# The stores of the results, issued from ScalarE's queue instead of SyncE's: a two-layer graph kernel on one Trainium2 core

## The chip, the cores and the metric

The kernel runs on one core of a Trainium2 chip. A core has five engines, each with an instruction queue of its own that is worked off in order: PE (TensorE, matrix products), DVE (VectorE), ACT (ScalarE), POOL (GpSimd) and SP (SyncE, which issues transfers and computes nothing). SP and ACT can both issue DMAs, and POOL issues the indirect ones. The metric is the device time of one execution in microseconds (us), lower is better.

## The reference

The input `x` has 32 batches of 512 channels by 1024 nodes, `adj` is 512 x 512, and everything is float32. Two graph layers follow each other, each with a residual and a normalisation over the nodes:

```python
q = einsum('c,bcn->bn', wq, x); k = einsum('c,bcn->bn', wk, x)
scores = leaky_relu(q[:, None, :] + k[:, :, None], 0.01)
att = softmax(scores, axis=-1)
agg = einsum('bcn,bmn->bcm', x, att)
x = layernorm(x + relu(einsum('oc,bcm->bom', adj, agg) + bm[None, :, None]))

W = support * adj            # as called here: adj * adj
x = layernorm(x + einsum('bnf,nm->bmf', x, W) + bias)
```

## The kernel before

The batches go through a software pipeline: in one pass of the list, `ld` works for the batch three ahead, `p`, `r`, `sd` and `fe` for the one two ahead, `t`, `e` and `pi` for the next, `u` and `m` for the current one, `st`, `av` and `so` for the one before. For one batch the steps are these; the short names are those of the kernel's own list.

- `ld0` to `ld3` (`load`, L131) bring the four channel tiles of x, 512 KB each, into one of three x buffers.
- `p0` to `p27` (`project`, L338) multiply x with the weights on PE; `k...` (`keep`) bring the products to `zrow`, on ACT or on DVE.
- The attention is not formed as a matrix. The scores depend on a sum of two numbers, so nodes are sorted by q: `r0` to `r7` (`place`, L403) count ranks on DVE, `sd` (`send`, L415) scatters the rows to their rank in a DRAM table `td` by indirect DMA on POOL, `fe` (`fetch`, L461 and L466) reads the sorted rows back into `zs`.
- `t0` to `t8` (`table`, L510) form running sums on PE, block by block. `e0` to `e8` (`table_out`, L522) copy each result out of PSUM on ACT. `ca` (on ACT) and `cp` (on POOL), both `carry` at L528, put the last row of a block into the next block, so that t(k+1) waits for e(k), ca(k) and cp(k). `ts` (`table_store`, L536) writes the sums back to the DRAM table from SP, two DMAs for each block.
- `pi` (`pick`, L543) gathers for each node its rows of the table, on POOL. `sc` (`scale`, L582) on ACT and `ga`, `gb` (`gain`, L587) on DVE mix them.
- `u`, `ad` (`add`, L603), `sq` (`square`, L611 and L612, on ACT), `rt` (POOL) and `y` (`finish`, L627 and L628, on ACT) turn the rows, add the residual and normalise.
- `m0` to `m13` (`multiply`, L676) are the second layer's products on PE, seven instead of eight by Strassen's scheme in Winograd's form, into the banks oA, oB and oC. `rd` (`read`, L697 and L699) brings them to `vall`, the one buffer for results in most rounds.
- `st`, `ro`, `sf` and `av` (`stats`, `root`, `shift`, `apply`, L705 to L729) normalise; `av0` to `av3` run on ACT, one for each of the four tiles of 128 x 1024. `so0` to `so3` (`store`, L734) write the four tiles to the output, 512 KB each. In the last batch, tiles 2 and 3 are normalised and stored in halves: `fa` (`apply_half`, half 0 on ACT, half 1 on DVE) and `fo` (`store_half`, L758).

The order of all this is written out by hand, as three lists of step names: BEGIN, SLOT and END. SLOT is run 28 times, each time with the roles moved on by one batch, and is called a round below. `with tc.manual_schedule()` keeps each engine's instructions in the order of the list; semaphores for data are added by the framework. In SLOT the stores stand here:

```python
k021 ga7 sc4 p19 sf1 gb1 e0 p17 ca0 ts0 sf2 cp0 sc6 x12 t1 av1 ga6 p16 gb6 e1 p18 wx1 cp1 ts1
ca1 wb1 p13 so1 k1p1 sc5 t2 ga4 gb7 p22 e2 x14 p23 ca2 k111 cp2 ga5 t3 k1u2 k1p5 gb5 p24 gb4 e3
ca3 u0 ts3 cp3 av2 so3 t4 ad0 so2 p21 so0 e4 ts2 ca4 u1 cp4 sq0 t5 ad1 p20 ld0 e5 ca5 u2 cp5 ts5
```

So in ACT's order the neighbours of so1 are ca1 and k1p1, and so3, so2 and so0 come one after the other between av2 and e4. In SP's order so1 stands between ts1 and ts3, and the other three between ts3 and ts2.

In the kernel before, all plain transfers are issued from SP, but for three small loads of vectors at the start (L76), which ACT issues.

Of the kernel before, what the change touches and what calls it, by code (L numbers as in the profile page):

```python
# [23 lines left out]
def gat_gcn_resnorm_kernel(  # L24
# [11 lines left out]
    nc = tc.nc  # L36
    P = 128
# [37 lines left out]
    for i, a in enumerate((wq, wk, bm)):  # L75
        nc.scalar.dma_start(  # L76
            out=vec[i * CT : (i + 1) * CT, :], in_=a.rearrange("(t p) -> t p", p=P)
# [9 lines left out]
    for half in range(2):  # L87
        p0 = half * G
        nc.gpsimd.affine_select(
            out=tri[p0 : p0 + G, 0, :], in_=tri[p0 : p0 + G, 0, :], pattern=[[-2, G]],  # L90
# [3 lines left out]
            out=tri[p0 : p0 + G, 1, :], in_=tri[p0 : p0 + G, 1, :], pattern=[[2, G]],  # L94
# [3 lines left out]
    for row, i in ((0, 0), (G, 1)):  # L98
# [14 lines left out]
        out=first, in_=first, pattern=[[-1, 2 * N - P]], compare_op=ALU.is_ge,  # L113
# [11 lines left out]
    xs, vs = {}, {}  # L125
# [16 lines left out]
    for td in tdb:  # L142
        nc.sync.dma_start(
            out=td.rearrange("(s u) c -> s u c", u=3)[N:NS, 0, :], in_=zs[P + N - NS : P, 0, 0:ZW]
        )
        odd = td.rearrange("(s w u) c -> s w (u c)", w=2, u=3)
        for r in range(0, NS // 2, P):
            n = min(P, NS // 2 - r)
            nc.sync.dma_start(
                out=odd[r : r + n, 0, ZW : 3 * ZW].rearrange("p (j c) -> p j c", j=2)[:, :, 0:1],  # L150
                in_=zs[0:n, 0:2, 1:2],
            )
            nc.sync.dma_start(
                out=odd[r : r + n, 1, ZW : 3 * ZW].rearrange("p (j c) -> p j c", j=2),
                in_=zs[0:n, 0:2, 0:ZW],
# [575 lines left out]
            by.tensor_scalar(t, t, rs, nb, ALU.mult, ALU.add)  # L731

    def store(b, mt):
        nc.sync.dma_start(out=out[b, mt * P : (mt + 1) * P, :], in_=vs[b][:, mt])  # L734

    parted = {}

# [17 lines left out]

    def store_half(b, mt, h):
        f = slice(h * H, (h + 1) * H)
        nc.sync.dma_start(out=out[b, mt * P : (mt + 1) * P, f], in_=vs[b][:, mt, f])  # L758

    steps = {}  # L760

# [38 lines left out]
    for ot in range(CT):  # L800
        also(0, f"u{ot}", turn, ot)
        also(0, f"ad{ot}", add, ot)
        also(0, f"sq{ot}", square, ot)
        also(0, f"rt{ot}", root0, ot)
        also(0, f"y{ot}", finish, ot)
        also(3, f"ld{ot}", load, ot)
        also(0, f"T{ot + 1}", less, ot + 1)
        also(-1, f"st{ot}", stats, ot)
        also(-1, f"ro{ot}", root, ot)
        also(-1, f"sf{ot}", shift, ot)  # L810
        also(-1, f"av{ot}", apply, ot)
        also(-1, f"so{ot}", store, ot)
# [8 lines left out]
    for mt in range(CT):  # L821
        also(0, f"ag{mt}", both, mt)
        for h in range(2):
            also(0, f"hb{mt}{h}", half, mt, h)
            also(0, f"fa{mt}{h}", apply_half, mt, h)
            also(0, f"fo{mt}{h}", store_half, mt, h)
# [150 lines left out]
```

## Time and profile before

| | |
|---|---|
| time, median of 3 runs | 2201.99 us (2200.96 to 2205.12) |
| the profiled execution | 2198.41 us |
| its span, first to last instruction | 2196.7 us |
| mean granted TensorE clock | 0.990 |
| HBM read, written | 338.17 MB, 208.30 MB |
| DMA queue q1 (SP) | 277.06 MB, 43.7% of 16 engines' span |
| DMA queue q0 (POOL) | 269.52 MB, 34.3% |
| DMA queue q10 (ACT) | 0.01 MB, 0.0% |

Times in the profile's lines are in us unless they are marked ns. In a timeline, a line has the start, the duration, the engine with the line of the kernel, the operation, what is written and read, how many instructions are merged, and in brackets the engine's idle time before it and who ended it. SPq and ACTq are the queues of these engines: issuing a DMA counts as no busy time of the engine. A DMA's duration there is that of the issue, not that of the transfer. L12 is line 12 of the kernel.

### The profile page before, as it was taken

What the parts mean: (1) busy time and instruction counts of PE and PEld (TensorE: products, weight loads), DVE (VectorE), ACT (ScalarE), POOL (GpSimd) and SP (SyncE); (2) the same over time, 40 slices, a digit from 0 to 9 for tenths busy, and PEclk for the clock granted to TensorE, in tenths of its full rate; (3) what the DMA queues carried; (4) which work ended last, traced back from release to release, by engine and by line L of the source; (5) the groups of instructions that cost most, each with busy time, mean ns of one, the idle gap of its engine ahead of it and who ended that gap; (6) DMA issues with size and microseconds to landing.
All of it is one profiled execution on the core that took longest, in us unless ns stands there. A gap on an engine that the chain in (4) does not pass through costs nothing.

```text
span 2196.7 us, 35479 instructions
## 1 busy us (share of the span) xinstructions
PE 2102.5 (96%) x11697; PEld 1222.4 (56%) x11697; DVE 1775.9 (81%) x3576; ACT 1652.8 (75%) x2758; POOL 987.6 (45%) x1291
## 2 busy tenths in 40 slices
PE   7879999999999999999999999999999999999877
PEld 5446555556555556555656555556655556655433
DVE  7567888888888888888888898888888888888666
ACT  1577777887777887777888777878777788777765
POOL 1344455444445444445443445544445544445442
PEclk9999999999999999999999999999999999999998
DMA  7567888878888777888777889887888887888752
GB/s 250 166 229 252 264 266 281 257 239 254 268 260 277 262 247 244 268 246 286 266 250 234 265 253 282 273 249 233 262 265 267 282 252 236 258 265 264 221 205 96
DMA packets 179152, 548.86 MB, mean 250 GB/s; under 512 B 27404, under 2 KB 27416, under 8 KB 178968
## 3 DMA queue, kind: packets, MB, share of 16 engines
q1 hardware_dynamic: 121600, 277.06, 43.7%
q0 software_dynamic: 57344, 269.52, 34.3%
q8 instruction: 93, 1.52, 0.3%
q14 instruction: 91, 0.75, 0.1%
q10 hardware_dynamic: 24, 0.01, 0.0%
HBM read 338.17 MB, written 208.30 MB: 249 GB/s over the span
## 4 chain that ended last, share of the span: by engine, by line
PE 62%; ACT 12%; DVE 10%; issue 6%; DMA 6%; POOL 3%; SPq 1%; DVEq 0%; POOLq 0%; ACTq 0%
PE zp_A L338 18%; PE tp L510 10%; PE oA L676 9%; PE zp_B L338 8%; PE op L596 5%; PE zp_C L338 4%; DVE junk L403 4%; ACT y L628 4%; PE oB L676 3%; PE oC L676 3%; DMA zs<-td 2%; ACT rows L582 2%; ACT v L699 1%; POOL zs L528 1%; DMA td<-zs 1%
## 5 line engine op out<-in xcount | busy, mean ns | idle before, releaser
L587 DVE SCALAR_TENSOR_TENSOR rows<-rows,ra 128x512 f32<-128x512 f32 x512 | 366.2, 739 | 20.9 <-ACT rows L582 17.6
L676 PE MATMUL oA<-y,adj_sb 128*128 128x512 f32 x768 | 356.6, 607 | 9.8 <-ACT y L628 6.3
L415 POOL DMA_INDIRECT td<-zrow,ranki x256 | 269.3, 1052 | 213.7 <-DVE idx L439 80.0
L510 PE MATMUL tp<-zs,lq 128*64 128x257 f32 x2304 | 335.1, 392 | 27.2 <-POOL zs L528 16.3
L543 POOL DMA_INDIRECT rows<-td,idx x256 | 297.1, 1160 | 88.1 <-issue 68.0
L403 DVE SCALAR_TENSOR_TENSOR junk<-qb,zrow,first 128x1024 int8<-128x1024 f32 x240 | 307.1, 1279 | 10.9 <-PE qb L376 4.2
L528 POOL COPY zs<-ts 1x513 f32<-1x513 f32 x128 | 93.2, 728 | 474.4 <-ACT ts L522 474.3
L338 PE MATMUL zp_A<-wb,x 128*64 128x257 f32 (+1 forms) x1536 | 278.9, 388 | 12.6 <-issue 3.5
L428 ACT ACTIVATE junk<-lq,kc 128x1024 int8<-128x1024 f32 x240 | 274.4, 1143 | 2.0
L603 DVE SCALAR_TENSOR_TENSOR y<-op,nbm,x 128x1024 f32<-128x1024 f32 x128 | 163.8, 1282 | 127.4 <-PE op L596 127.2
L676 PEld LDWEIGHTS oA<-y,adj_sb 128*128 128x128 f32 x768 | 144.7, 193 | 191.7 <-issue 153.8
L510 PEld LDWEIGHTS tp<-zs,lq 128*64 128x64 f32 x2304 | 168.7, 136 | 135.6 <-POOL zs L528 37.8
L582 ACT ACTIVATE rows<-rows,ra 128x512 f32<-128x512 f32 x256 | 180.1, 718 | 77.5 <-DVE den L574 39.5
L359 ACT COPY zrow<-zp_A 128x514 f32<-128x514 f32 x192 | 112.8, 588 | 147.4 <-PE zp_A L338 130.1
L338 PEld LDWEIGHTS zp_A<-wb,x 128*64 128x64 f32 (+1 forms) x1536 | 177.0, 155 | 77.3 <-issue 25.1
L528 POOL COPY zs<-zs 1x513 f32<-1x513 f32 x128 | 78.3, 611 | 253.0 <-ACT zs L522 253.0
L628 ACT ACTIVATE y<-y,nb,r 128x1024 f32<-128x1024 f32 x128 | 158.9, 1241 | 4.3
L705 DVE BATCH_NORM_STATS2 st<-v 128x6 f32<-128x512 f32 x240 | 151.9, 674 | 0.0
L612 ACT ACTIVATE x<-y,nm 128x1024 f32<-128x1024 f32 x128 | 147.2, 1150 | 4.2
L729 ACT ACTIVATE v<-v,nb,rs 128x1024 f32<-128x1024 f32 x120 | 148.1, 1234 | 2.3 <-DVE nb L721 1.4
L596 PE MATMUL op<-ident,rows 128*128 128x128 f32 x1024 | 141.2, 282 | 4.6 <-DVE rows L587 2.6
L596 PEld LDWEIGHTS op<-ident,rows 128*128 128x128 f32 x1024 | 114.9, 143 | 46.1 <-issue 24.6
(162 smaller groups left out, 3784.6 us busy)
## 6 DMA issues: line engine op xcount, KB each, us to landing
x<-in_x_dram SPq DMA_DIRECT2D x128, 512.0 KB
out_dram<-v SPq DMA_DIRECT2D x120, 512.0 KB
zs<-td SPq DMA_DIRECT2D x64, 602.3 KB
td<-zs SPq DMA_DIRECT2D x288, 120.2 KB
td<-ts SPq DMA_DIRECT2D x224, 120.2 KB
zs<-td SPq DMA_DIRECT2D x64, 240.9 KB
zs<-td SPq DMA_DIRECT2D x96, 120.5 KB
td<-zs SPq DMA_DIRECT2D x8, 514.0 KB
```

Source lines behind the costliest of these rows:

```text
L338: nc.tensor.matmul(zp[n : n + wide, m, 0:CE], side(b, g, a)[:, c, m * P + n : m * P + n + wide], wb[:, w, c, :], start=first and c == 0, s ...
L403: nc.vector.scalar_tensor_tensor(junk(b)[:, 0:N], qbs[b], zrow[:, nt, 0:1], first[:, o : o + N], ALU.subtract, ALU.is_lt, accum_out=rank[: ...
L415: sc = nc.gpsimd.indirect_dma_start(out=td[:, :], out_offset=bass.IndirectOffsetOnAxis(ap=ranki[:, nt : nt + 1], axis=0), in_=zrow[:, nt, ...
L428: nc.scalar.activation(junk(b)[:, N : 2 * N], qs[b], AF.Sign, bias=kcs[b][:, nt : nt + 1], accum_out=signs(b)[:, nt : nt + 1],)
L510: nc.tensor.matmul(tp[i * G : (i + 1) * G, h, 0:CE], lw[:, ks[i], :], zs[:, j, 1 + h * CE : 1 + (h + 1) * CE], start=True, stop=True,)
L528: copy(zs[row : row + 1, to, 1:ZW], ts[row : row + 1, 0 : ZW - 1])
L543: nc.gpsimd.indirect_dma_start(out=rows[:, mt, :], out_offset=None, in_=tdb[b % 2].rearrange("(s u) c -> s (u c)", u=3), in_offset=bass.In ...
L582: nc.scalar.activation(u, u, AF.Copy, scale=ratios(b)[:, k, 1:2])
L587: nc.vector.scalar_tensor_tensor(u, rg[:, k, i, 1 : C + 1], ratios(b)[:, k, i : i + 1], u, ALU.mult, ALU.add)
L596: nc.tensor.transpose(op[:, mt * P : (mt + 1) * P], rg[:, mt, 1, 1 + ot * P : 1 + (ot + 1) * P], ident)
L628: nc.scalar.activation(yall[:, ot], yall[:, ot], AF.Identity, bias=nb, scale=r)
L676: nc.tensor.matmul(o[:, m, :], quarters[w][:, a, m * P : (m + 1) * P], part(b, y)[:, a, :], start=fresh and a == 0, stop=a == CT // 2 - 1, ...
```

## The change

The results' stores are issued by ACT instead of SP. They keep their places in the list, and so stand in ACT's order of instructions where they stood in SP's. What is stored, from where and in which pieces stays the same.

```diff
     def store(b, mt):
-        nc.sync.dma_start(out=out[b, mt * P : (mt + 1) * P, :], in_=vs[b][:, mt])
+        nc.scalar.dma_start(out=out[b, mt * P : (mt + 1) * P, :], in_=vs[b][:, mt])
...
     def store_half(b, mt, h):
         f = slice(h * H, (h + 1) * H)
-        nc.sync.dma_start(out=out[b, mt * P : (mt + 1) * P, f], in_=vs[b][:, mt, f])
+        nc.scalar.dma_start(out=out[b, mt * P : (mt + 1) * P, f], in_=vs[b][:, mt, f])
```

## The prediction

> **What bounds the kernel now.** I read the page first, then the chain of waits, then the busy time of each engine by stage in one round (a round is one pass of SLOT; a new one starts about every 65 us), and then the timelines of the four engines around the stores.
>
> ```profile
> PE 2102.5 (96%) x11697; PEld 1222.4 (56%) x11697; DVE 1775.9 (81%) x3576; ACT 1652.8 (75%) x2758; POOL 987.6 (45%) x1291
> ...
> PE 62%; ACT 12%; DVE 10%; issue 6%; DMA 6%; POOL 3%; SPq 1%; DVEq 0%; POOLq 0%; ACTq 0%
> ```
>
> The first line says that PE has work for 96% of the span. The second says that only 62% of the chain that ended last is PE: elsewhere the chain runs over ACT and DVE and comes back to PE. So the question is not whether ACT, at 75%, has room on average, but whether it has room where the stores stand in the list. The busy times by stage answer that (columns: window, its length, busy us of PE, PEld, DVE, ACT, POOL, clock, DMA share, GB/s).
>
> ```profile
> 1110.00:1120.00 10.00, 9.87 (x89) 6.36 (x86) 8.23 (x14) 9.09 (x17) 3.03 (x4) 1.00 0.31 105
> 1120.00:1132.00 12.00, 12.00 (x92) 8.37 (x90) 6.54 (x11) 10.91 (x19) 3.32 (x7) 1.00 0.88 300
> 1132.00:1140.00 8.00, 8.00 (x35) 4.15 (x35) 7.25 (x18) 7.78 (x13) 4.40 (x6) 1.00 0.79 226
> ...
> sum 65.00, PE 64.53 PEld 37.55 DVE 54.52 ACT 51.52 POOL 30.69; mean PE 12.91 PEld 7.51 DVE 10.90 ACT 10.30 POOL 6.14
> ```
>
> The four stores of a round are issued at 1113.95, 1120.00, 1121.08 and 1121.49. From 1110 to 1140 ACT is busy for 27.8 of 30 us, and PE idles 0.47 us in the whole round. That 0.47 us is also all that any change outside PE can win per round. The chain of waits shows where ACT's time becomes PE's, here two rounds earlier:
>
> ```profile
> 1009.92 1.24 ACT y L628
> 1011.16 0.29 ACT nb L627
> 1011.48 1.25 ACT y L628
> 1012.72 0.04 issue
> 1012.77 2.84 PE oC L676 x6
> ```
>
> PE starts oC 0.04 us after the last `finish`. Whatever ACT is late by when it reaches this point, PE loses.
>
> **The change, part by part.** *Removed from SP:* 126 issues of `store` and 4 of `store_half`, at a median of 0.364 us. SP issues 34 DMAs a round, some 34 x 0.4 = 14 of 65 us, and then waits for the scatter (766 us over the span before the fetch, L461), so the time saved there is spare. Behind the stores on SP stand the table stores ts2 and ts5 to ts8 and the x loads. They may go 1 to 2 us earlier. Nobody waits for them there: the x tile is read by the next round, and the first gather that needs the table rows starts at 1074.17 in the round before, 0.30 us after POOL has finished issuing a scatter. I take 0 and keep a gain of 0.30 us a round as the bound.
>
> *Moved to ACT:* the same four issues, and the waits that they carry. The timelines of SP and of ACT and POOL around the last three of them:
>
> ```profile
> 1120.00 0.38 SPq L734 DMA_DIRECT2D out_dram<-v  x1
> 1121.08 0.36 SPq L734 DMA_DIRECT2D out_dram<-v  x1
> 1121.49 0.46 SPq L734 DMA_DIRECT2D out_dram<-v  x1
> ```
>
> ```profile
> 1119.82 1.24 ACT L729 ACTIVATE v<-v,nb,rs 128x1024 f32<-128x1024 f32 x1
> 1121.47 0.59 ACT L522 COPY zs<-tp 128x514 f32<-128x514 f32 x1 [0.41 <-PE tp L510]
> 1122.09 0.62 ACT L528 COPY zs<-zs 1x513 f32<-1x513 f32 x1
> ...
> 1124.40 0.59 ACT L522 COPY zs<-tp 128x514 f32<-128x514 f32 x1 [0.20 <-PE tp L510]
> ...
> 1127.32 0.59 ACT L522 COPY zs<-tp 128x514 f32<-128x514 f32 x1 [0.17 <-PE tp L510]
> ```
>
> ```profile
> 1122.12 0.61 POOL L528 COPY zs<-zs 1x513 f32<-1x513 f32 x1 [2.21 <-ACT zs L522]
> ```
>
> so1 (1113.95) reads a part that was finished 1.4 us earlier; on ACT it stands behind ca1 (0.61 us), which covers an issue of 0.36 us if the queue runs ahead of the engine. Without that cover, ACT's idle time of 0.24 and 0.46 us within the next 4 us takes it. Price 0. so3 stands behind av2, 1.24 us of cover for 0.38 us; price 0, or 0.38 us where the issue cannot run beside av2. so2 reads what av2 writes: it can start only at 1121.06, as it does on SP now. There the wait is harmless; on ACT it holds so0, then e4 (`table_out`, 1121.47), ca4, sq0, e5 and all that follows. so2 and so0 take from 1121.06 to 1121.95; with 0.10 us to restart, e4 begins at 1122.05, 0.58 us late.
>
> Who waits for e4: the carries on ACT and POOL, and then t5 on PE.
>
> ```profile
> 1122.25 1.03 PE L596 MATMUL op<-ident,rows 128*128 128x128 f32 x8
> 1123.21 1.09 PE L510 MATMUL tp<-zs,lq 128*64 128x257 f32 x8
> ```
>
> POOL's carry ends at 1122.73 and t5 starts at 1123.21, a slack of 0.48 us, and I read the same 0.49 us in nearly every round. So t5 is late by about 0.1 us. On ACT the 0.58 us shrinks by the idle 0.20 us before e5 and 0.17 us before e6, to 0.21 us, or to 0.29 us if 0.04 us of each gap is handoff that stays. I take 0.25. From 1127.3 ACT has no gap until `finish`, and PE waits there: 0.25 us a round. 28 rounds of SLOT give 7.0 us.
>
> What can move that: the issue's length. Nothing in the trace shows a 512 KB store from ACT. The nearest rows are SP's stores, and ACT's three small loads at the start:
>
> ```profile
> L734 SPq DMA_DIRECT2D out_dram<-v x120: 332/364/2046, 199.2 to 2174.9; - x120
> ```
>
> ```profile
> 0.80 0.57 ACTq L76 DMA_DIRECT2D v<-in_L_gnn_wq_dram  x1
> 1.40 0.26 ACTq L76 DMA_DIRECT2D v<-in_L_gnn_wk_dram  x1
> 1.69 0.31 ACTq L76 DMA_DIRECT2D v<-in_L_gnn_bm_dram  x1
> ```
>
> At 0.26 and 0.31 us, 0.25 us less for the pair, the round loses nothing. At 0.57 us each, 0.32 us more, it loses 0.57 us: 16 us. With so3 exposed as well, 0.95 us: 27 us. I take SP's own rows, the same transfer. Their maximum is 2.05 us: in 5 of 27 rounds I read so0 at 0.74 to 2.05 us, 5.2 us above the median in all; on SP nothing suffers, on ACT it would be added whole. Table stores share SP's queue, and ACT's would hold the stores alone, so I count half, 2.6 us.
>
> *END:* the last ten stores go to ACT's list between `apply` and `apply_half`. fa20 would start behind so1's issue, some 0.4 us late; but the last `apply_half` waits for DVE now, and SP's last four issues (2.23 us in a row, to 2190.49) are then spread between them. 0 to 0.5 us; 0.4.
>
> Sum: 7.0 + 2.6 + 0.4 = 10.0 us. The profiled execution took 2198.41 us (span 2196.7, 1.7 outside it), 3.6 us under the median of 2201.99; the same 10 us on the median give 2212.
>
> Two pages of the Trainium skill point opposite ways. "DMA: Bandwidth & Descriptors", section "Issuing engines are not separate DMA queues", says that queues of different engines feed the same 16 DMA engines and that a second issuing engine saves only issue time; by it the transfers gain nothing, and the sum stands. "Perfetto Trace Analysis", section "DMA Optimizations", advises one issuing engine for inputs and another for outputs; if that held here, the sum would lose its sign.
>
> **The rivals.** *Dearer issue:* ACT's issue is like its first row (0.57 us), or the engine must be empty before it: +16 to +27 us, 2218 to 2229. For it: that first row; against: its two followers at 0.26 and 0.31 us, and that SP was issuing in the same 0.57 us.
>
> *Hidden:* the issue costs 0.3 us, or ACT's gaps take more than I allow: 0 to 4 us, 2202 to 2206. For it: the slack of 0.49 us before t5 and 0.78 us of idle ACT within 6 us; against: the gapless ACT from 1127.3 on.
>
> *Faster:* 1.5 MB of stores no longer stand ahead of table rows and x loads in one queue; the rows land earlier, and the gather, which now starts 0.30 us after POOL is free, starts earlier. It decides if those 0.30 us are a wait for table rows and the gather is on the path. 28 x 0.30 = 8.4 us: 2194. Against it: the stores are issued by 1121.95 and the last table rows of a round about 14 us later, and a scatter's issue ends just before the gather.
>
> That the change does not do what it says is no rival: the list fixes the order, and the two edits name the queue.
>
> **How the numbers follow.** Forecast 0.42, dearer 0.20, hidden 0.24, faster 0.14. A measurement of this kernel tells about 0.2% (4.4 us) from no change. Slower by more: 0.42 + 0.20 + 0.01 of the hidden case = 0.63; same 0.23; faster 0.14. The likeliest is 2212; its own range is 2207 to 2218. The range reaches from 2197, which leaves out most of the faster case, to 2230, just past the dear end: about 0.15 lies outside.
>
> **What would show it.** Right: 130 store rows at ACTq and none at SPq; ACT's second queue carries some 67 MB that SP's loses; e4 starts about 0.6 us after t4's end, e6 about 0.25 us later than now behind t6; the waits of PE for POOL's carry (tp) and for `finish` (oC) grow, and the rounds are 0.25 us longer. Wrong: e4 still starts 0.1 us behind t4 (the issue is hidden), ACT store rows of 0.6 us or more (dearer), or a gather that starts earlier against r7's rank with PE idle less than 0.47 us a round (faster).

## The result, and the profile after

The changed kernel took 2209.45 us (median of 22 runs, 2204.18 to 2218.21); the kernel before took 2201.84 us beside it (22 runs, 2198.62 to 2210.81). The ratio is 1.0034, 95% interval 1.0024 to 1.0043: 7.6 us slower, 5.3 to 9.5. The profiled execution took 2210.35 us, its span is 2208.6 us.

The same two lines of the page as before, busy time and the shares of the chain that ended last:

```profile
PE 2104.3 (95%) x11697; PEld 1218.8 (55%) x11697; DVE 1774.3 (80%) x3576; ACT 1649.8 (75%) x2758; POOL 987.5 (45%) x1291
...
PE 57%; ACT 14%; DVE 10%; DMA 6%; issue 6%; POOL 4%; ACTq 1%; SPq 1%; DVEq 0%; POOLq 0%
```

No engine has more work than before; the busy times differ by 4 us at most. What changed is the chain: PE's share falls from 62% to 57%, ACT's rises from 12% to 14%, POOL's from 3% to 4%, and ACTq, the issuing on ACT, appears with 1%. The lost time is time in which PE waits for something that now runs over ACT. The pages of the experiments below bear this out: PE has 55 to 57% of the chain in the three kernels of 83.5 us and more in the table further down (e4_two_more apart), and 62 to 67% in the ten of 79.9.

The stores are where the list has them, in ACT's queue (first the groups of these rows, then two queues with packets, MB and share of the 16 engines' span):

```profile
L734 ACTq DMA_DIRECT2D out_dram<-v x120: 338/367/473, 200.2 to 2187.8; - x120
L734 ACTq DMA_DIRECT2D out_dram<-x x6: 338/338/789, 2186.0 to 2199.5; - x6
```

```profile
q1 hardware_dynamic: 102880, 209.95, 36.5%
...
q10 hardware_dynamic: 18744, 67.12, 8.2%
```

On ACT an issue costs 0.367 us at the median, on SP it was 0.364. But the longest of these 120 is 0.473 us, where SP had rows of up to 2.046 us: the long issues of the rounds are gone. One of the six in the second row, from the last section, took 0.789 us, as one of them did on SP (0.788).

The busy times by stage, the three windows of before moved on by 7.9 us (columns as before):

```profile
1117.90:1127.90 10.00, 9.86 (x89) 6.28 (x86) 8.23 (x14) 9.08 (x17) 3.04 (x4) 1.00 0.34 104
1127.90:1139.90 12.00, 11.96 (x91) 8.30 (x89) 6.54 (x11) 10.71 (x19) 3.31 (x7) 1.00 0.91 298
1139.90:1147.90 8.00, 8.00 (x34) 4.14 (x34) 7.15 (x18) 7.79 (x14) 4.35 (x6) 1.00 0.77 219
```

For PE and ACT only the middle window differs: ACT is busy for 10.71 instead of 10.91 us, and PE, which had no idle time in it, has 0.04. The timelines of ACT, POOL and PE show why:

```profile
1128.98 0.83 ACTq L734 DMA_DIRECT2D out_dram<-v  x2
1129.91 0.59 ACT L522 COPY zs<-tp 128x514 f32<-128x514 f32 x1 [0.96 <-PE tp L510]
...
1135.32 0.59 ACT L522 COPY zs<-tp 128x514 f32<-128x514 f32 x1
```

```profile
1130.56 0.60 POOL L528 COPY zs<-zs 1x513 f32<-1x513 f32 x1 [2.75 <-ACT zs L522]
```

```profile
1131.21 1.09 PE L510 MATMUL tp<-zs,lq 128*64 128x257 f32 x8
```

av2 ends at 1128.95; so2 and so0 are issued until 1129.81; `e4` starts at 1129.91, after 0.96 us of idle ACT where there were 0.41. The bracket still names t4 on PE, but that had ended 0.67 us before: the wait is the two issues. POOL's carry ends at 1131.16 and t5 starts 0.05 us later. Before, 0.48 us lay between them. The chain of waits, one round later, has the issues in it (start, length, what):

```profile
1192.76 1.25 ACT v L729
...
1194.03 0.36 ACTq L734
...
1194.42 0.46 ACTq L734
...
1194.98 0.60 ACT zs L522
...
1195.63 0.61 POOL zs L528
...
1196.29 1.09 PE tp L510 x8
```

This is the whole mechanism in six lines: av2, the two issues, `e4`, the carry on POOL, t5 on PE. Asked for the 4 us up to t5 alone, the chain goes over a store's issue in 25 of 27 rounds; in the kernel before it did in none.

How much it costs can be read without scatter. From the first matmul of t4 to the first of t5 every one of 27 rounds took 2.96 us before and 3.07 to 3.11 us after (one round 3.26). The table gives the sums over these rounds, and the rest of the rounds, for all kernels of this study; "gather" is the last section's first gather, explained under the experiments.

| kernel | t4 to t5, 27 rounds | rest of the 27 rounds | gather late | ratio to before |
|---|---|---|---|---|
| before | 79.9 | 1684.5 | no | |
| after | 83.6 | 1688.1 | yes | 1.0034 [1.0024, 1.0043] |
| e1_round_only | 83.6 | 1688.2 | no | 1.0029 [1.0018, 1.0039] |
| e2_end_only | 79.9 | 1684.6 | yes | 1.0012 [0.9999, 1.0025] |
| e3_so2_late | 79.9 | 1684.8 | yes | 1.0010 [0.9998, 1.0021] |
| e4_two_more | 150.3 | 1702.4 | yes | 1.0425 [1.0408, 1.0441] |
| e5_so2_alone | 79.9 | 1685.3 | no | 0.9995 [0.9983, 1.0008] |
| e6_no_stores | 79.9 | 1691.4 | no | 1.0004 [0.9992, 1.0017] |
| e7_so0_first | 79.9 | 1689.4 | yes | 1.0013 [1.0002, 1.0023] |
| e8_late_end_sp | 79.9 | 1687.3 | no | 0.9995 [0.9983, 1.0007] |
| e9_end_so0_late | 79.9 | 1687.1 | no | 0.9991 [0.9977, 1.0005] |
| e10_after_end_so0_late | 83.5 | 1692.6 | no | 1.0019 [1.0007, 1.0031] |
| e11_end_cured | 79.9 | 1688.7 | no | 1.0003 [0.9993, 1.0014] |
| e12_end_control | 79.9 | 1689.3 | yes | 1.0010 [0.9999, 1.0022] |

The first column is exact to 0.1 us. The second, e4_two_more apart, differs by up to 8 us, and by 4.7 us between e2_end_only and e12_end_control, which are the same kernel; so nothing under some 5 us can be read from it in one trace. Each group of kernels has its own runs of before, on the same chip: e1 to e4 (2199.93 us), e5 to e8 (2201.27), e9 and e10 (2204.64), e11 and e12 (2203.27).

### The profile page after: what moved, and what is told of

It reads as the page before. It is cut to its first block, busy times and chain, and to the rows that moved or that the text cites. A ratio compares the mean times of both kernels' runs of the same rounds, so it can differ in the third digit from the quotient of the medians.

```text
span 2208.6 us, 35388 instructions
## 1 busy us (share of the span) xinstructions
PE 2104.3 (95%) x11697; PEld 1218.8 (55%) x11697; DVE 1774.3 (80%) x3576; ACT 1649.8 (75%) x2758; POOL 987.5 (45%) x1291
## 4 chain that ended last, share of the span: by engine, by line
PE 57%; ACT 14%; DVE 10%; DMA 6%; issue 6%; POOL 4%; ACTq 1%; SPq 1%; DVEq 0%; POOLq 0%
PE zp_A L338 16%; PE oA L676 11%; PE tp L510 8%; PE zp_B L338 7%; PE zp_C L338 4%; DVE junk L403 4%; PE oB L676 4%; ACT y L628 3%; PE oC L676 3%; PE op L596 3%; DMA zs<-td 3%; POOL zs L528 2%; ACT v L729 1%; DMA td<-zs 1%; ACT ts L522 1%
## 5 line engine op out<-in xcount | busy, mean ns | idle before, releaser
L510 PE MATMUL tp<-zs,lq 128*64 128x257 f32 x2304 | 336.3, 393 | 32.5 <-POOL zs L528 15.6
L543 POOL DMA_INDIRECT rows<-td,idx x256 | 297.1, 1161 | 91.7 <-issue 65.1
L612 ACT ACTIVATE x<-y,nm 128x1024 f32<-128x1024 f32 x128 | 147.1, 1149 | 4.1
```

Source lines behind the costliest of these rows:

```text
L510: nc.tensor.matmul(tp[i * G : (i + 1) * G, h, 0:CE], lw[:, ks[i], :], zs[:, j, 1 + h * CE : 1 + (h + 1) * CE], start=True, stop=True,)
L543: nc.gpsimd.indirect_dma_start(out=rows[:, mt, :], out_offset=None, in_=tdb[b % 2].rearrange("(s u) c -> s (u c)", u=3), in_offset=bass.In ...
```

## The experiments

**Which part of the list pays?** The stores on ACT in the 28 rounds alone, then in the last ten stores (END) alone.

```diff
 def store(b, mt):
+    by = nc.scalar if b < B - 4 else nc.sync     # e1_round_only; e2_end_only: b >= B - 4
-    nc.scalar.dma_start(...)
+    by.dma_start(...)
```

In e1_round_only `store_half`, which is only in END, goes back to SP too.

> Stores of batches 0 to 27, those of the 28 rounds of SLOT, are issued by ACT; the sixteen stores and half stores of END by SP as before. Theory A (ACT's queue: so2 waits for av2, and the issues of so2 and so0 hold e4, so that t5 on PE is late): the repeated round is 65.07 us as in the changed kernel, against 64.95 us before, so at least 28 x 0.12 = 3.4 us of the measured 7.5 us; time 2205 to 2207. Theory C (the loss sits in END, where ACT is on the chain and PE's clock is halved after gaps): no change of the total, 2202. Theory B (a second queue with 67 MB makes the transfers of the other queues late, wherever the stores stand): nearly all of the 7.5 us, 2209.

> Only the stores of the last four batches, those in END, are issued by ACT; those of SLOT by SP as before. Theory A: the repeated round is 64.95 us as before, and the total is 0 to 2 us above the kernel before. Theory C: 4 to 7 us above it. Theory B: below 1 us, 4 of 32 batches.

e1_round_only took 2206.96 us, ratio 1.0029 [1.0018, 1.0039]; e2_end_only 2202.70 us, 1.0012 [0.9999, 1.0025]. The two parts, 0.29% and 0.12%, add up to 0.41%, and the change was 0.34% (0.24 to 0.43): within the intervals they make up the whole. The rounds pay most of it. END pays some 2.6 us, more than the 0.4 us of the prediction and than the 0 to 2 us expected here, though its interval alone still touches 1.

**Is it the place in ACT's list?** All stores stay on ACT, and only so2 and so0 leave the place between av2 and `e4`.

```diff
-    ca3 u0 ts3 cp3 av2 so3 t4 ad0 so2 p21 so0 e4 ts2 ca4 u1 cp4 sq0 t5 ad1 ...
+    ca3 u0 ts3 cp3 so3 so0 av2 t4 ad0 p21 e4 ts2 ca4 u1 cp4 sq0 so2 t5 ad1 ...
```

> All stores on ACT, as in the changed kernel, but in SLOT so3 and so0 stand before av2, and so2 stands after sq0, so that no store waits for an instruction that ACT has just been given. Theory A: all four issues are hidden beside running instructions, e4 starts 0.08 us after t4 again with 0.4 us of idle ACT before it, the slack between the carry and t5 is back at 0.49 us, the round is 64.95 us, and of the 7.5 us only END's part is left: 2202 to 2205. Theory B: same queue and same bytes, so no better than the changed kernel, 2209. If ACT's issues cost the engine time by themselves, 1.5 us a round would stay visible as idle time before ACT instructions.

It took 2203.08 us, ratio 1.0010 [0.9998, 1.0021]. The timeline of ACT:

```profile
1121.83 1.24 ACT L729 ACTIVATE v<-v,nb,rs 128x1024 f32<-128x1024 f32 x1 [0.48 <-issue]
1123.03 0.59 ACT L522 COPY zs<-tp 128x514 f32<-128x514 f32 x1
...
1124.54 0.34 ACTq L734 DMA_DIRECT2D out_dram<-v  x1
```

Not every issue is hidden: av2 is 0.48 us late behind the issue of so0. But that uses up the idle 0.41 us that ACT had between av2 and `e4`, and `e4` starts 1.21 us after the first matmul of t4, as in the kernel before (1.76 in the changed kernel). so2 is issued at 1124.54, 0.01 us after the start of a `square` (L612, 1.15 us) that covers it. t4 to t5 is back at 2.96 us in every round. The same four issues on the same engine cost PE nothing there: the price was the place, not the engine. What is left, 0.10%, is about that of e2_end_only, and both have the late gather.

**More of the same cost.** so2 and so0 in two halves each, at their places in the changed kernel.

```diff
 def store(b, mt):
+    if b < B - 4 and mt in (0, 2):
+        for h in range(2):
+            f = slice(h * H, (h + 1) * H)
+            nc.scalar.dma_start(out=out[b, mt * P : (mt + 1) * P, f], in_=vs[b][:, mt, f])
+        return
```

> As the changed kernel, but in the 28 rounds so2 and so0 are each issued as two halves of 128 x 512, so that two more issues stand between av2 and e4; the bytes are the same. Theory A: e4 is 0.56 + 2 x 0.40 = 1.36 us later than in the kernel before, the slack of 0.44 us is used up already, so the whole 0.8 us reaches t5: a round of 65.9 us, 28 x 0.8 = 22 us more than the changed kernel, 2231. Theory B: within 2 us of the changed kernel, 2209 to 2211.

It took 2294.18 us, ratio 1.0425 [1.0408, 1.0441], far more than two more issues of 0.4 us can explain. ACT and then PE in one round:

```profile
1170.15 3.25 ACTq L737 DMA_DIRECT2D out_dram<-v  x4
1173.50 0.59 ACT L522 COPY zs<-tp 128x514 f32<-128x514 f32 x1 [3.38 <-issue]
```

```profile
1174.81 1.98 PE L510 MATMUL tp<-zs,lq 128*64 128x257 f32 x8 [2.46 <-POOL zs L528]
```

The four issues took 0.367, 0.457, 1.220 and 1.100 us (medians of the 28 rounds 0.36, 0.46, 1.27 and 1.07). so3 had been issued 1.9 us earlier, so the third of the four is the fourth store in the queue within 3 us. PE waits 2.46 us for the carry, and the matmuls behind that wait are slower as well: t5 takes 1.98 us instead of 1.09, and the granted clock of the 2 us from 1174.8 is 0.50. Against the changed kernel, t4 to t5 takes 66.7 us more over the 27 rounds, the rest of them 14.3. The path is the one of the theory; the size was missed because an issue's length is not a constant, and because the granted clock is lower behind the longer wait. Halves carry half the bytes over the same 128 rows, and it is their number that costs. On SP, ts2, right behind three stores in the kernel before, took 1.107 and 1.139 us for its two issues in one round (medians 1.12 and 1.15), and 0.41 and 0.41 in e6_no_stores below. But the stores need not be in the same queue: in the changed kernel, with no store on SP, they are 1.09 and 0.58.

**The wait for av2, apart from the issues.** Only so2 on ACT, all others on SP.

```diff
 def store(b, mt):
+    by = nc.scalar if mt == 2 and b < B - 4 else nc.sync
```

> In the 28 rounds of SLOT only so2 is issued by ACT; so1, so3, so0 and all of END stay on SP. Theory A: so2 still waits for av2 in ACT's queue, but one issue of 0.37 us behind it makes e4 only 0.1 us later than in the kernel before, less than the 0.44 us of slack before t5; round 64.95 us, no stall at t5, time equal to before within 0.1%. If the wait for av2 on ACT's queue were the cost by itself, the round would be 65.05 us or more and the time 3 to 7 us above before.

2201.23 us, ratio 0.9995 [0.9983, 1.0008]; t4 to t5 at 2.96 us. The wait for av2 with one issue behind it fits into the slack. It takes the second issue to overrun it.

**Is there anything to win on SP or on the DMA engines?** The kernel before, with stores of the last four batches only.

```diff
 def store(b, mt):
+    if b >= B - 4:
         nc.sync.dma_start(...)
```

> The kernel before without the stores of batches 0 to 27: 112 of the 128 result tiles are computed and not written. It shows what all these stores cost where they were, on SP, and so the most that moving them could have won. Theory A: nothing, the round stays 64.95 us; 0 to 3 us less in all. The rival of the prediction that the stores hold up table rows and x loads in SP's queue: 8 us less, 2192, and a gather that starts up to 0.3 us earlier.

2201.58 us, ratio 1.0004 [0.9992, 1.0017]. With 59 MB of stores gone altogether the kernel is not faster: by the interval, at most 0.08% or 1.8 us. On SP they cost next to nothing, so moving them can win next to nothing.

**so0 alone out of the way.** All stores on ACT; so0 moves ahead of av2, so3 and so2 stay behind it.

```diff
-    ca3 u0 ts3 cp3 av2 so3 t4 ad0 so2 p21 so0 e4 ts2 ca4 ...
+    ca3 u0 ts3 cp3 so0 av2 so3 t4 ad0 so2 p21 e4 ts2 ca4 ...
```

> All stores on ACT; in SLOT so0 alone is moved, from behind so2 to before av2, so that av2, so3, so2 follow each other and one issue instead of two stands between the end of av2 and e4. Theory A: e4 0.1 us late, covered by the slack; round 64.95 us; total as with so2 placed late, 0 to 3 us above before. If three issues in a row fill ACT's queue wherever they stand, so2's issue grows over 0.5 us and the round stays above 65.05 us.

2204.80 us, ratio 1.0013 [1.0002, 1.0023]; t4 to t5 at 2.96 us. One issue between av2 and `e4` is free, as in e5_so2_alone. The 0.13% is of the size of END's, and the gather is late here too.

**Both cures of what was known by then.** The list of e3_so2_late in the rounds, END's stores on SP.

> SLOT with the stores on ACT and so3, so0 before av2 and so2 after sq0; the stores of END on SP as before. Theory A: no loss is left anywhere; 1.000 of the time before, within 0.1%, a round of 64.95 us, END (from the last oC of SLOT to the end) 205 to 207 us against 208 us with END's stores on ACT. A gain below 0.999 would show that freeing SP's queue is worth something once ACT pays nothing.

2200.58 us, ratio 0.9995 [0.9983, 1.0007]: the loss is gone, and nothing is gained over before. END took 205.1 us in its profile, as expected.

**What END pays for.** The last batch's first gather (`pick`, L543, on POOL) waits for ts8, the last table store of SP. POOL before and after (the bracket is POOL's idle time ahead of the gather, and what ended it):

```profile
2117.38 1.15 POOL L543 DMA_INDIRECT rows<-td,idx  x1 [1.49 <-DVE y L603]
```

```profile
2127.71 1.15 POOL L543 DMA_INDIRECT rows<-td,idx  x1 [2.71 <-DMA out_dram<-v]
```

and ACT after:

```profile
2122.80 0.37 ACTq L734 DMA_DIRECT2D out_dram<-v  x1
...
2129.83 0.29 ACT L627 ACTIVATE nb<-nm,r 128x1 f32<-128x1 f32 x1 [1.41 <-POOL r L620]
```

Before, so0 of batch 29 stands behind ts8 in SP's order and is issued at 2114.24, after it; ts8's rows landed at 2115.94, ahead of it. After, nothing holds ACT back: it issues so0 at 2122.80, 0.12 us before SP issues the last piece of ts8 (2122.92). The store's 512 KB then take the DMA engines (in 2124 to 2125 us ACT's queue is at 86% and 320 GB/s, SP's at 15% and 32 GB/s), and ts8 lands at 2126.66. POOL's bracket names the store; but POOL passes the wait at 2126.69, and the store's own last part lands at 2127.10, so it is ts8 that holds the gather. The gather is late, POOL's root behind it is late, `finish` waits 1.41 us for the root (0.18 before), and PE for `finish`, between the second and the third of the next eight matmuls. PE before and after:

```profile
2119.37 6.19 PE L676 MATMUL oA<-y,adj_sb 128*128 128x512 f32 x8 [1.74 <-ACT y L628]
```

```profile
2128.48 2.07 PE L676 MATMUL oA<-y,adj_sb 128*128 128x512 f32 x2 [1.61 <-ACT y L628]
2131.45 5.45 PE L676 MATMUL oA<-y,adj_sb 128*128 128x512 f32 x6 [0.90 <-ACT y L628]
```

Three kernels test this by moving only that store behind the gather:

```diff
-    @31 sh @29 so0 @30 sq1 rt0 ad2 @31 sx @30 ad3 sq2 @31 pi0 @30 sA
+    @31 sh @30 sq1 rt0 ad2 @31 sx @30 ad3 sq2 @31 pi0 @29 so0 @30 sA
```

in e3_so2_late (e9), in the changed kernel (e10), and in e2_end_only (e11, with e2_end_only itself once more beside it, e12).

> All stores on ACT, the rounds as in e3_so2_late, and in the last section the store so0 of batch 29 moved behind the last batch's first gather (pi0). Theory A (the remaining loss of the stores on ACT in END comes from one store that ACT issues before SP has issued the table store ts8, so that ts8 lands late and holds the first gather): ts8 lands within 2 us of its last issue, the first gather no longer waits for it, finish no longer waits 1.4 us for POOL's root, END takes 205 to 206 us instead of 207.5, ratio to before 0.9990 to 1.0005. Theory B (the loss in END is the other nine stores' issues on ACT, or PE's clock): END stays at 207 to 208 us, ratio about 1.0010, as in e3_so2_late.

> The changed kernel with that one store of END moved, nothing else. Theory A: the rounds keep their 7 us (the sum over 27 rounds stays 7 to 8 us above before), END returns to 205 to 206 us: ratio 1.0025 to 1.0032, as e1_round_only (1.0029). Theory B: nothing changes against the changed kernel: 1.0034 to 1.0040.

> Only the stores of END on ACT (the 28 rounds as before), and batch 29's so0 moved behind the last batch's first gather. If the late gather is the whole loss of END: ratio to before 0.9993 to 1.0005 and 1.5 to 2.5 us below the control on the same chip; the gather waits about 1.4 us for DVE as before. If the loss is spread over the other nine issues: within 0.7 us of the control, ratio 1.0007 to 1.0015.

> The control on the same chip: the kernel of e2_end_only once more, with the stores of END on ACT at their old places. Both theories: ratio 1.0007 to 1.0015, the first gather waits 2.7 us and comes 1.2 us late.

The ratios are 0.9991 [0.9977, 1.0005], 1.0019 [1.0007, 1.0031], 1.0003 [0.9993, 1.0014] and 1.0010 [0.9999, 1.0022]. In e11_end_cured POOL's line is that of before again:

```profile
2123.26 1.15 POOL L543 DMA_INDIRECT rows<-td,idx  x1 [1.41 <-DVE y L603]
```

From the last matmul of the table to the sixth of these eight, PE falls behind the kernel before by 1.22 to 1.27 us in the changed kernel, e2_end_only, e3_so2_late, e7_so0_first and the control, and by nothing in all three with the store moved (-0.04). That step is shown. Its size in the whole time is less sharp. These eight matmuls ran at a granted clock of 0.51 in the changed kernel and e3_so2_late, 0.59 in the kernel before, e2_end_only and the control, and 0.55 to 0.56 in the three with the store moved; with that, PE is 2.2, 1.0 to 1.1 and 0.3 to 0.4 us behind the kernel before when they are done. So the clock adds to the wait or takes from it in one trace and another, and what sets it there was not tested. Every kernel with the store moved has a lower ratio than its counterpart, and in the one pair on the same chip it is 2.1 us faster (2203.55 and 2205.67 us), but the intervals of each pair overlap. As for the length of END that was expected of e9 and e10: it was 208.8 and 207.3 us in their profiles, against 205.4 before and 208.1 after, so it did not fall to 205 to 206; but one profile's END says little, as e1_round_only, whose END is that of before, took 206.9. e9's END had lost 2.9 us ahead of the gather already, e10's 1.3. Nor did e10 keep to the rest of what was expected: its ratio is under the 1.0025 to 1.0032, and its 27 rounds took 11.7 us more than before in its one profile, not 7 to 8, which is within the scatter of the table. These two ran on a chip on which the kernel before also took 2204.64 us, which may be why; it wasn't settled.

## Why the prediction was right, and where its sum was not

The forecast was 2212 us, slower; measured were 2209.45. Up to t5 the mechanism is the one described: the queue, the rows and the megabytes are as listed, `e4` is 0.55 us late against the 0.58 of the sum, and the slack ahead of t5 is used up. From there on it is not: the rounds lose by another way than the sum says, the long issues cost nothing, and END pays for something that was not foreseen. That 10.0 came near 7.6 is in part luck.

*The rounds, 7.0 us.* The step that failed is "On ACT the 0.58 us shrinks ... I take 0.25". ACT's own lateness does shrink so: `e5` is 0.26 us late in the round shown. But `e6` waits for t6 (it starts 1.19 us after t6's first matmul, before and after), and behind `e6` everything up to oC keeps its distance to it (14.32 us in every round, before and after, to 0.01). So the sign that was listed, `e6` 0.25 us later behind t6 and a round longer by 0.25 us, did not come: it was 0.00 and some 0.12. `e6` was 0.11 us late, because t5 and t6 were, and ACT's remainder of 0.26 less 0.17 us of idle time is less than that. What a round loses is t5's delay, which the prediction had worked out as "about 0.1 us" and then not used: 0.48 us of slack against 0.58. Summed over the rounds it is 3.7 us in 27, so 3.8 in 28. e1_round_only measured 6.4 us (4.0 to 8.6) for the rounds; the change less e3_so2_late (0.24%) and e10 less e9 (0.28%) give 5 to 6 us. So some 2 us may lie elsewhere in the rounds. PE's waits ahead of oC sum to 8.9 to 10.1 us over the 27 rounds in the three kernels of 83.5 us and more in the table, e4_two_more apart, and to 6.4 to 8.6 in those of 79.9, which is a hint and no more. From t5 to oC and from the next t0 to t4 all thirteen kernels agree to 3 us over the 27 rounds; the scatter is between oC and the next t0, where the ten kernels of 79.9 took 860.0 to 866.8 us and the three others 862.8 to 868.3. So if these 2 us are there, they are in that stretch, and what makes them stays open.

*Long issues, 2.6 us.* Nothing: the longest issue on ACT in the rounds took 0.473 us, and the half that I counted did not come over. That SP's long ones were due to the table stores in its queue was argued and is not shown. e4_two_more shows that ACT's queue has long ones as well, once four stores come close together.

*END, 0.4 us.* About 2.3 us, by the ratios 1.0010 to 1.0013 of the kernels that pay only there, three of the four with an interval that touches 1. I had looked at the issues that stand between ACT's steps, and at what comes earlier on SP, but not at what a store on its own queue may run ahead of.

*Waits.* The 0.47 us that the prediction took as the most a round can win is the idle time of PE in one round; over the 27 rounds it is 20.8 us, 0.77 a round. PE's wait for `finish` at oC grew, as listed, from 5.3 to 7.8 us over the span. The wait for POOL's carry did not grow in the list of waits (16.3 us before, 15.6 after): it is full of waits at t0 and t1, and what t5 lost was slack, and then 0.1 us a round.

3.8 and 2.3 make 6.1 us, inside the 5.3 to 9.5 that were measured; 10.0 was above it. Errors of both signs have partly cancelled.

*The rivals.* Dearer issue: no, 0.338 to 0.473 us on ACT in the rounds, and so1 and so3 are issued beside a running instruction. Hidden: in the rounds it came nearest, 3.8 us of the 0 to 4 it allowed; END and the small remainder carried the total out of it. Faster: no. e6_no_stores without the stores is at 1.0004 and e8_late_end_sp with them out of the way of both engines at 0.9995.

Of the two pages of the Trainium skill that pointed opposite ways, "DMA: Bandwidth & Descriptors", section "Issuing engines are not separate DMA queues", fits this kernel: by the same two ratios the transfers gained nothing. What "Perfetto Trace Analysis", section "DMA Optimizations", says may make sense, an engine of their own for outputs, won nothing here. END has a row for another section of the first page, "Two DMAs through the same engine are not ordered": within one queue of a DMA engine descriptors start in order, and across the 16 engines nothing orders DMAs. On SP, so0 was issued behind ts8 in the same queue, and ts8 landed at 2115.94, ahead of the first part of so0 at 2116.78; on a queue of its own so0 was no longer held.

No version beat the kernel before; e5_so2_alone, e8_late_end_sp, e9_end_so0_late and e11_end_cured equal it.

## What to carry to other kernels

In these runs a DMA issue on ACT was free as far as it ran beside an instruction of ACT (0.37 us beside a copy of 0.62), and it came on top where it had to wait for the instruction just before it (two issues, `e4` 0.55 us late, after 0.41 us of idle time had been used up). So look at what stands next in that engine's order, add up the issues behind the wait, and compare them with the slack of the next thing that the busiest engine waits for. Then follow the delay on the engine that is the bound, not on the one that was held up. And a queue of its own also takes away an order: look for the transfers that the moved one used to stand behind, and for who waits for them.

## What the runs showed of the hardware that I had not expected

- Three stores of 128 rows are issued one after the other at 0.34 to 0.47 us each; the next issue in that queue, within 3 us, took 1.27 us at the median on ACT (e4_two_more) and 1.12 on SP (ts2 in the kernel before). Halving the bytes did not help. It is not a matter of one queue alone: with the stores in ACT's queue, the first issue of ts2 on SP still took 1.09 us at the median, and without stores 0.41. What the limit is was not tested.
- ACT issues a DMA while its own instruction is running (so3 at 1127.07, 0.01 us after the start of a 0.62 us copy), unless the DMA reads what a running instruction writes (so2 at 1128.98, 0.03 us after av2's end).
- A 512 KB store issued 0.12 us ahead of the last 98 KB of table rows (48 rows of 2052 bytes) delayed their landing from 1.74 to 3.35 us after the end of their last issue.
